# A decoder layer on one core: six state tiles instead of four, three decay tiles instead of two, and an earlier product for dt

## The chip, the core and the metric

The kernel runs on one core of a Trainium2 chip. The core has a matrix engine (PE, with its weight loads listed as PEld), a vector engine (DVE), a scalar engine (ACT), a general engine (POOL) and a queue that issues transfers (SP). Each engine works through its own list of instructions in a fixed order, and an instruction that waits holds up everything behind it on that engine. The metric is the device time of one execution in microseconds (us), the median over runs. One further execution was profiled; it gives the lines that are shown.

## The reference

Eight sequences of 512 tokens with 512 features go through three layers, each followed by a layer norm over the features:

```
x = layernorm(x + mamba(x));  x = layernorm(x + cross_attention(x, ctx));  x = layernorm(x + mixture_of_experts(x))
mamba: xn = layernorm(x);  x_main, z = split(xn @ in_proj)            # 1024 channels each
       x_main = silu(causal_conv4(x_main));  dt, Bm, Cm = split(x_main @ x_proj)      # 32, 16, 16 columns
       dt = softplus(dt @ dt_proj + b)
       h[t] = exp(A * dt[t]) * h[t-1] + dt[t] * Bm[t] * x_main[t]     # 16 states for each channel, over all t
       out = ((sum over states of h * Cm) + x_main * D) * silu(z) @ out_proj * res_scale + x
experts: a gate picks 4 of 32 experts for each token; every expert has room for 640 tokens
```

Attention has 16 heads of 32. All data are 32-bit floats.

## The kernel before

The program has three parts in a row: `layers` (the recurrent layer, attention, the gate and the shared expert, until about 4,000 us of the profiled span), `experts` and `finish`. The change is in `layers` alone.

`layers` walks over 16 chunks: 8 sequences, each in two halves of 256 tokens (`T`). A chunk has 32 steps: four pairs of channel tiles (`q`, 128 channels to a tile), for each pair four groups of four states (`g`), for each of these the two channel tiles of the pair (`ci`). One step handles 128 channels, four states and 256 tokens, and its work is spread over the engines:

- `carry` (L443, ACT) takes a state tile `h` and writes the last value of the chunk before into its first column. Tag "h" has four buffers.
- `decays` (L437, ACT) writes exp(A*dt) for the *next* step into one of the decay tiles `das`. There are two, used in turn, so the decays for step k+1 wait until the scan of step k-1 has read that tile.
- `scan` on DVE: a product dt*x*B into `h` (L449), the scan along the tokens in place (L453), and for a first half a copy of the last column (L455).
- `collect`: the product with C on DVE (L470), and on PE eight matmuls that add the states into the accumulator `py` (L474). When these are done, the buffer of `h` is free for a later step.

For every pair, `prepare` makes what its steps need: two matmuls for dt (L392) into a PSUM tile of tag "mm" (two buffers, shared by nearly all matmul results), then on ACT the parts of softplus (L402 to L408), on DVE four operations (L412 to L415), and eight DMAs on SP that spread dt and dt*x over the partitions into the two `both` tiles (L426). In the loop `prepare` for the next pair is called in step 3 of a pair (`k % 8 == 3`), and for the next chunk in step 27.

Around the steps stand, in program order: `gated` (L486, DVE, needs the finished `py` of the pair before) in the first step of a pair; `twice_x` (L490) in step 0, which loads x for the residual; `back` in steps 1 and 2 (output projection of the chunk before, residual and layer norm); `gate_x` in steps 3 to 6; for the next chunk `load_x` (L274) in step 5, `norm_x` (statistics L73, L74, then L54 to L77) in step 9, `flip_x` in step 11, `convolve` in steps 12, 15, 18 and 21 (first tap on ACT, L331, the other three taps on DVE, L339), silu (L356, L357) in step 23 and `x_proj` in step 24. The tile that `load_x` fills and the tile of `twice_x` have the same tag "xt" with one buffer. Between these, pieces of attention, gate and shared expert of the sequence before (`units`, with the score matmuls L766 and L792, the row maximum L768 on DVE and the exponentials L796 on ACT) are dealt out by weight, so that they end with the two chunks of a sequence.

The order that each engine finally sees is not the program order. A scheduler takes instructions by priority (program order) as their inputs and their tiles come free in its own model of the times, and writes one fixed list for each engine. A change of buffers or of a call's place therefore reorders all of `layers`. Below, "the built order" is this list.

Of the kernel before, what the change touches and what calls it, by code (L numbers as in the profile page):

```python
# [7 lines left out]
F32 = mybir.dt.float32  # L8
# [73 lines left out]
def layers(ctx, tc, a, x1d, filld, based, xbuf):  # L82
# [53 lines left out]
    cw = const("cw", [P, CC, 4], rows(a["conv_w"]))  # L136
    cb = const("cb", [P, CC], a["conv_b"])
    w_x = const("w_x", [P, CC, RANK + 2 * NST], rows(a["x_proj_w"]))
    w_dt = const("w_dt", [RANK, DI], a["dt_proj_w"])
    b_dt = const("b_dt", [P, CC], a["dt_proj_b"])  # L140
    dpar = const("dpar", [P, CC], a["D_param"])
    rs = const("rs", [P, 1], a["res_scale"].partition_broadcast(P))
# [15 lines left out]
    state = cp.tile([P, CC, NST // NG, NG], F32, name="l_state")  # L158
    nothing = cp.tile([P, NG, 1], F32, name="l_nothing")
    nc.gpsimd.memset(nothing, 0.0)  # L160
    das = [cp.tile([P, NG, T + 1], F32, name=f"l_da{i}") for i in range(2)]
    for da in das:
        nc.gpsimd.memset(da[:, :, 0:1], 0.0)

# [23 lines left out]
        channel_multiplier=0,  # L188
    )

    early = cp.tile([P, SC, E], F32, name="l_early")
    nc.gpsimd.iota(
        early, pattern=[[0, SC], [-1, E]], base=E, channel_multiplier=0, allow_small_or_imprecise_dtypes=True
    )
    first = cp.tile([P, SC, E], F32, name="l_first")
    nc.gpsimd.iota(
        first, pattern=[[0, SC], [CAP, E]], base=-SLOTS, channel_multiplier=0, allow_small_or_imprecise_dtypes=True
    )

    taken = cp.tile([P, SC + 1, E], F32, name="l_taken")  # L200
    nc.gpsimd.memset(taken, 0.0)
# [67 lines left out]

    piece = pieces()  # L270

    def load_x(b, t, f):
        f["xt"] = xt = p1.tile([P, NT_, D], F32, tag="xt", name="xt")
        nc.sync.dma_start(xt, a["x"][b, t * T : (t + 1) * T, :].rearrange("(j p) d -> p j d", p=P))  # L274
# [39 lines left out]
    def convolve(t, q, f):  # L314

        c0 = 2 * q
        ps = project(f, "ps_x")

        def first_tap():
            xp = p1.tile([P, 2, T + 3], F32, tag="xp", name="xp")  # L320
            if t == 0:
                nc.gpsimd.memset(xp[:, :, 0:3], 0.0)
            else:
                nc.gpsimd.tensor_copy(xp[:, :, 0:3], conv_tail[:, c0 : c0 + 2, :])
            nc.scalar.copy(xp[:, :, 3:], ps)
            if t < S // T - 1:
                nc.gpsimd.tensor_copy(conv_tail[:, c0 : c0 + 2, :], xp[:, :, T : T + 3])
            f["xs"][q] = xs = p2.tile([P, 2, T], F32, tag="xs", name="xs", bufs=6)
            for i in range(2):
                c = c0 + i  # L330
                nc.scalar.activation(  # L331
                    xs[:, i, :], xp[:, i, 0:T], AF.Identity, bias=cb[:, c : c + 1], scale=cw[:, c, 0:1]
                )

            def other_taps():
                for i in range(2):
                    acc = xs[:, i, :]
                    for k in range(1, 4):
                        nc.vector.scalar_tensor_tensor(  # L339
                            acc, xp[:, i, k : k + T], cw[:, c0 + i, k : k + 1], acc, ALU.mult, ALU.add  # L340
                        )

            return other_taps

        return first_tap
# [40 lines left out]

    def prepare(q, f):

        ps = psm.tile([P, 2, T], F32, tag="mm", name="ps_dt")
        for i in range(2):  # L390
            c = 2 * q + i
            nc.tensor.matmul(  # L392
                ps[:, i, :], w_dt[:, c * P : (c + 1) * P], f["xd"][0:RANK, :], start=True, stop=True
            )

        def exponentials():
# [5 lines left out]
                nc.scalar.activation(u[:, i, :], ps[:, i, :], AF.Abs, bias=b_dt[:, c : c + 1])  # L402
                nc.scalar.activation(dt[:, i, :], ps[:, i, :], AF.Relu, bias=b_dt[:, c : c + 1])
            nc.scalar.activation(u, u, AF.Exp, scale=-1.0)
            l = p1.tile([P, 2, T], F32, tag="l", name="l")
            nc.scalar.activation(l, u, AF.Ln, bias=1.0)
            w = dtx = p1.tile([P, 2, T], F32, tag="dtx", name="dtx")
            nc.scalar.activation(w, u, AF.Identity, bias=1.0)  # L408
# [30 lines left out]
    def carry(t, c, g):  # L439

        last = state[:, c, g].unsqueeze(2)
        h = p3.tile([P, NG, T + 1], F32, tag="h", name="h", bufs=4)
        nc.scalar.copy(h[:, :, 0:1], last if t else nothing)  # L443
        return h

# [40 lines left out]
        nc.vector.tensor_tensor(pair, pair, py, ALU.mult)  # L486

    def twice_x(b, t, f):
        f["o"] = o = p1.tile([P, NT_, D], F32, tag="xt", name="o")
        nc.sync.dma_start(o, a["x"][b, t * T : (t + 1) * T, :].rearrange("(j p) d -> p j d", p=P))  # L490
        nc.scalar.mul(o, o, 2.0)

# [51 lines left out]
    def choose(b, x2t, pl, st):  # L544
# [13 lines left out]
        square = [P, SC, G, G]  # L558
        other = gs.unsqueeze(2).to_broadcast(square)
        own = gs.unsqueeze(3).to_broadcast(square)  # L560
        eq = gm.tile(square, F32, tag="g_eq", name="g_eq")
        nc.vector.tensor_tensor(eq, other, own, ALU.is_equal)
        nc.vector.tensor_tensor(eq, eq, lower.unsqueeze(1).to_broadcast(square), ALU.mult)
        gt = gm.tile(square, F32, tag="g_gt", name="g_gt")
        nc.vector.tensor_tensor(gt, other, own, ALU.is_gt)
        nc.vector.tensor_tensor(gt, gt, eq, ALU.add)
        nc.vector.tensor_reduce(rank.unsqueeze(3), gt, AX.X, ALU.add)
# [455 lines left out]
    for i, (b, t) in enumerate(chunks):  # L1023
# [8 lines left out]
        for k, (q, g, ci) in enumerate(steps):  # L1032
# [6 lines left out]

            if k + 1 < len(steps) or after:  # L1040
                nq, ng, ni = steps[(k + 1) % len(steps)]
                decays(2 * nq + ni, ng, (f if k + 1 < len(steps) else nf)["ready", nq][0], das[(n + 1) % 2])
            scan(t, 2 * q + ci, g, f["ready", q][1], bc, das[n % 2], h)
            n += 1
            if k % 8 == 0:
                if k:
# [10 lines left out]
            if k == 7:  # L1057
                dry()
                silu(f["zs"])
            if k % 8 == 3:  # L1060
                if q + 1 < CC // 2:
                    do(prepare, q + 1, f)
                elif after:
                    do(prepare, 0, nf)
            if after:
                if k == 5:
                    load_x(*after, nf)
                if k == 9:
                    norm_x(nf)
# [349 lines left out]
```

## Time and profile before

| | |
|---|---|
| median of 3 runs | 5617.29 us (5615.69 to 5618.11) |
| profiled execution, its own time | 5620.06 us |
| its span, first to last instruction | 5617.3 us |
| mean clock granted to PE | 0.934 |
| busy over the span: PE, DVE, ACT, POOL | 87%, 77%, 46%, 10% |
| 512 steps on DVE, mean of one: L449, L453, L470 | 1.22, 2.30, 1.22 us |

In the profile's lines an operation is given by its line in the kernel, engine, names of the tiles (output <- inputs), shapes and count; after a bar follow its busy time, the mean of one in ns, and the idle time of the engine just before it with what ended it. In the chain of waits, a line such as "DVE h L449 <- PE py L474" means that the DVE instruction of L449 stood waiting, and that the PE instruction of L474 released it; then come the total in us, the number of times and the longest.

### The profile page before, as it was taken

The page shows a single profiled execution, that of the slowest core. Times are in us where ns is not written, and L with a number is a line of the kernel's source. Part 1 is how long each engine was busy: PE and PEld are TensorE (multiplying, and loading weights), DVE is VectorE, ACT ScalarE, POOL GpSimd, SP SyncE. Part 2 cuts the span into 40 slices and gives each one's busy share as a digit, 9 for nine tenths or more (in the row PEclk, how much of TensorE's full clock was granted, in tenths as well). Part 3 has the DMA queues.
Part 4 walks back from the last instruction along what each step waited for, and adds up shares of the span by engine and source line. Part 5 has one row for each costly group of instructions (what it writes and reads, how often), then busy time and mean ns, then how long its engine had stood idle before and what let it go on. Part 6 is the DMA issues. An engine that isn't in the chain of part 4 may idle for free. (4 is left out here: it accounts for less than half of the span.)

```text
span 5617.3 us, 60406 instructions
## 1 busy us (share of the span) xinstructions
PE 4888.6 (87%) x19752; PEld 2725.6 (49%) x19752; DVE 4351.5 (77%) x5738; ACT 2592.2 (46%) x5480; POOL 546.1 (10%) x424
## 2 busy tenths in 40 slices
PE   5667888888888988888888898879899999999994
PEld 3333344434433434443443443333577777777773
DVE  5988888989889998898989899854555655555554
ACT  4454555655556555565545656523122222222223
POOL 0000002001100200200010020010111111111111
PEclk8778999999999999999999999989899999999997
DMA  6777345434534534543463453431444444444444
GB/s 207 215 219 201 99 129 177 128 112 130 189 107 113 190 107 122 177 132 106 124 204 94 125 183 110 115 118 45 137 124 126 124 124 119 125 126 124 120 117 138
DMA packets 560426, 769.83 MB, mean 137 GB/s; under 512 B 135754, under 2 KB 268394, under 8 KB 560112
## 3 DMA queue, kind: packets, MB, share of 16 engines
q1 hardware_dynamic: 522608, 680.70, 40.2%
q0 software_dynamic: 33280, 76.90, 7.0%
q10 hardware_dynamic: 4224, 8.39, 0.4%
q8 instruction: 156, 2.56, 0.2%
q14 instruction: 158, 1.29, 0.1%
HBM read 508.68 MB, written 165.05 MB: 120 GB/s over the span
## 5 line engine op out<-in xcount | busy, mean ns | idle before, releaser
L437 ACT ACTIVATE l_da<-both,l_aneg 128x256 f32<-128x256 f32 x2048 | 888.4, 499 | 801.8 <-DVE h L453 759.7
L453 DVE TENSOR_TENSOR_SCAN h<-l_da,h 128x1028 f32<-128x1028 f32 x512 | 1171.2, 2295 | 48.5 <-ACT h L443 26.4
L474 PE MATMUL py<-h,l_twice 128*64 128x256 f32 x4096 | 628.1, 420 | 217.4 <-DVE h L470 217.3
L449 DVE TENSOR_TENSOR h<-both,bc 128x1024 f32<-128x1024 f32 x512 | 619.2, 1216 | 97.2 <-PE py L474 45.4
L470 DVE TENSOR_TENSOR h<-h,bc 128x1024 f32<-128x1024 f32 x512 | 623.5, 1220 | 6.0
L474 PEld LDWEIGHTS py<-h,l_twice 128*64 128x64 f32 x4096 | 295.3, 147 | 587.6 <-DVE h L470 260.7
L766 PE MATMUL ps_s<-l_ka,l_qa 64*128 64x512 f32 x1024 | 317.1, 699 | 142.9 <-DVE mx L768 142.7
L1199 PE MATMUL ps_h<-xT,w 128*128 128x320 f32 x1536 | 435.6, 433 | 0.0
L1279 POOL DMA_INDIRECT based<-y,xe x160 | 250.5, 1565 | 1317.2 <-ACT y L1302 579.9
L768 DVE TENSOR_REDUCE mx<-ps_s 128x2 f32<-128x1024 f32 x256 | 310.8, 1217 | 83.7 <-PE ps_s L766 82.9
L1220 DVE TENSOR_TENSOR hT<-ps_h,p 128x320 f32<-128x320 f32 x128 | 62.9, 492 | 374.7 <-PE ps_h L1199 374.6
L1199 PEld LDWEIGHTS ps_h<-xT,w 128*128 128x128 f32 x1536 | 292.4, 191 | 118.4 <-issue 0.8
L792 PE MATMUL ps_t<-l_qa,l_ka 64*128 64x512 f32 x1024 | 302.0, 654 | 15.8 <-ACT eT L796 11.9
L796 ACT ACTIVATE eT<-ps_t 128x1024 f32<-128x1024 f32 x256 | 259.1, 1013 | 111.9 <-PE ps_t L792 111.5
L808 PE MATMUL po<-eT,l_va 128*64 128x512 f32 x1024 | 279.2, 623 | 23.0 <-ACT raw L820 19.0
L1199 PE MATMUL ps_h<-t,s 128*128 128x320 f32 x1024 | 286.1, 432 | 0.0
L641 POOL DMA_INDIRECT xbuf<-x2t,dest x128 | 216.7, 1693 | 622.1 <-DVE dest L635 583.7
L305 PE MATMUL ps_z<-xnT,wm 128*128 128x256 f32 x1024 | 246.3, 395 | 31.2 <-DMA wm<-in_in_proj_w 28.4
L503 PE MATMUL po<-wm,zs 128*128 128x512 f32 x512 | 246.7, 634 | 13.0 <-DMA wm<-in_out_proj_w 8.5
L703 PE MATMUL ps_p<-x2T,wa 128*128 128x512 f32 x512 | 244.7, 627 | 11.1 <-DVE hT L883 9.1
L305 PE MATMUL ps_x<-xnT,wm 128*128 128x256 f32 x1024 | 245.3, 393 | 1.4 <-ACT xnT L294 1.1
L305 PEld LDWEIGHTS ps_z<-xnT,wm 128*128 128x128 f32 x1024 | 196.2, 196 | 83.7 <-ACT l_da L437 27.1
(225 smaller groups left out, 7397.0 us busy)
## 6 DMA issues: line engine op xcount, KB each, us to landing
bc<-scr SPq DMA_DIRECT2D x1024, 128.0 KB
w<-in_w SPq DMA_DIRECT2D x96, 1024.0 KB
wm<-in_in_proj_w SPq DMA_DIRECT2D x128, 512.0 KB
xbuf<-zero SPq DMA_DIRECT2D x32, 1362.5 KB
xe<-xbuf SPq DMA_DIRECT2D x32, 1362.5 KB
both<-dt SPq DMA_DIRECT2D x256, 128.0 KB
both<-dtx SPq DMA_DIRECT2D x256, 128.0 KB
wm<-in_out_proj_w SPq DMA_DIRECT2D x64, 512.0 KB
```

Source lines behind the costliest of these rows:

```text
L305: nc.tensor.matmul(ps[:, i, :], w[:, dc, i * P : (i + 1) * P], f["xnT"][:, dc, :], start=(dc == 0), stop=(dc == DC - 1),)
L437: nc.scalar.activation(da[:, n, 1:], dt[:, c % 2, j, :], AF.Exp, scale=aneg[:, c, j, g, m : m + 1])
L449: nc.vector.tensor_tensor(steps, dtx[:, c % 2].unsqueeze(2).to_broadcast([P, 2, NG // 2, T]), bc[0], ALU.mult)
L453: nc.vector.tensor_tensor_scan(flat, da.rearrange("p n t -> p (n t)"), flat, 0.0, ALU.mult, ALU.add)
L470: nc.vector.tensor_tensor(steps, steps, bc[1], ALU.mult)
L474: nc.tensor.matmul(py[j * HP : (j + 1) * HP, c % 2, :], twice, h[:, j * 2 + m, 1:], start=False, stop=(s == (NST // NG - 1, NG // 2 - 1, 1)),)
L766: nc.tensor.matmul(ps[:, j, :], qa[r, lt * P : (lt + 1) * P], ka[r, :], start=True, stop=True)
L768: return lambda: nc.vector.tensor_reduce(mx[:, lt, :].unsqueeze(2), ps, AX.X, ALU.max) and None
L792: nc.tensor.matmul(ps[:, j, :], ka[r, kc * P : (kc + 1) * P], qa[r, :], start=True, stop=True)
L796: nc.scalar.activation(eT, ps, AF.Exp)
L808: nc.tensor.matmul(po[j * 2 * HD : (j + 1) * 2 * HD, :], va[:, kc, i, j * HD : (j + 2) * HD], eT[:, j, :], start=(kc == 0), stop=(kc == SC ...
L1199: nc.tensor.matmul(ps, w[:, n, r * P : (r + 1) * P], x[:, n, :], start=not more and n == 0, stop=n == 1, skip_group_check=more,)
```

## The change

- `h` has six buffers, `das` three tiles.
- `twice_x` uses a tile of its own (tag "o"), so that x for the next chunk and x for the residual no longer share one.
- `prepare` for the next pair is called in the first step of a pair (0, 8, 16), and for the next chunk in step 26; `load_x` in step 3.
- The weights for dt are no longer held in SBUF as a whole. A generator loads the 32x256 piece for a pair, one pair ahead, into two buffers: 65 DMAs on SP instead of one.
- To make room: `xs` (the convolved x) has five buffers instead of six; the tile `l` of softplus shares its one buffer with `xp`, the input of the convolution; two tiles of the gate share the buffers of tag "row"; two constant tables of the gate are kept once and read repeatedly.

```diff
@@ -136,7 +136,6 @@
     cw = const("cw", [P, CC, 4], rows(a["conv_w"]))
     cb = const("cb", [P, CC], a["conv_b"])
     w_x = const("w_x", [P, CC, RANK + 2 * NST], rows(a["x_proj_w"]))
-    w_dt = const("w_dt", [RANK, DI], a["dt_proj_w"])
     b_dt = const("b_dt", [P, CC], a["dt_proj_b"])
     dpar = const("dpar", [P, CC], a["D_param"])
     rs = const("rs", [P, 1], a["res_scale"].partition_broadcast(P))
@@ -158,7 +157,7 @@
     state = cp.tile([P, CC, NST // NG, NG], F32, name="l_state")
     nothing = cp.tile([P, NG, 1], F32, name="l_nothing")
     nc.gpsimd.memset(nothing, 0.0)
-    das = [cp.tile([P, NG, T + 1], F32, name=f"l_da{i}") for i in range(2)]
+    das = [cp.tile([P, NG, T + 1], F32, name=f"l_da{i}") for i in range(3)]
     for da in das:
         nc.gpsimd.memset(da[:, :, 0:1], 0.0)
 
@@ -188,14 +187,12 @@
         channel_multiplier=0,
     )
 
-    early = cp.tile([P, SC, E], F32, name="l_early")
-    nc.gpsimd.iota(
-        early, pattern=[[0, SC], [-1, E]], base=E, channel_multiplier=0, allow_small_or_imprecise_dtypes=True
-    )
-    first = cp.tile([P, SC, E], F32, name="l_first")
-    nc.gpsimd.iota(
-        first, pattern=[[0, SC], [CAP, E]], base=-SLOTS, channel_multiplier=0, allow_small_or_imprecise_dtypes=True
-    )
+    early = cp.tile([P, E], F32, name="l_early")
+    nc.gpsimd.iota(early, pattern=[[-1, E]], base=E, channel_multiplier=0, allow_small_or_imprecise_dtypes=True)
+    early = early.unsqueeze(1).to_broadcast([P, SC, E])
+    first = cp.tile([P, E], F32, name="l_first")
+    nc.gpsimd.iota(first, pattern=[[CAP, E]], base=-SLOTS, channel_multiplier=0, allow_small_or_imprecise_dtypes=True)
+    first = first.unsqueeze(1).to_broadcast([P, SC, E])
 
     taken = cp.tile([P, SC + 1, E], F32, name="l_taken")
     nc.gpsimd.memset(taken, 0.0)
@@ -269,6 +266,19 @@
 
     piece = pieces()
 
+    def dts():
+
+        got = None
+        for n in range(B * (S // T) * CC // 2 + 1):
+            q = n % (CC // 2)
+            nxt = p2.tile([RANK, 2 * P], F32, tag="wdt", name="wdt")
+            nc.sync.dma_start(nxt, a["dt_proj_w"][:, 2 * q * P : 2 * (q + 1) * P])
+            if got is not None:
+                yield got
+            got = nxt
+
+    w_dt = dts()
+
     def load_x(b, t, f):
         f["xt"] = xt = p1.tile([P, NT_, D], F32, tag="xt", name="xt")
         nc.sync.dma_start(xt, a["x"][b, t * T : (t + 1) * T, :].rearrange("(j p) d -> p j d", p=P))
@@ -325,7 +335,7 @@
             nc.scalar.copy(xp[:, :, 3:], ps)
             if t < S // T - 1:
                 nc.gpsimd.tensor_copy(conv_tail[:, c0 : c0 + 2, :], xp[:, :, T : T + 3])
-            f["xs"][q] = xs = p2.tile([P, 2, T], F32, tag="xs", name="xs", bufs=6)
+            f["xs"][q] = xs = p2.tile([P, 2, T], F32, tag="xs", name="xs", bufs=5)
             for i in range(2):
                 c = c0 + i
                 nc.scalar.activation(
@@ -386,11 +396,11 @@
 
     def prepare(q, f):
 
+        w = next(w_dt)
         ps = psm.tile([P, 2, T], F32, tag="mm", name="ps_dt")
         for i in range(2):
-            c = 2 * q + i
             nc.tensor.matmul(
-                ps[:, i, :], w_dt[:, c * P : (c + 1) * P], f["xd"][0:RANK, :], start=True, stop=True
+                ps[:, i, :], w[:, i * P : (i + 1) * P], f["xd"][0:RANK, :], start=True, stop=True
             )
 
         def exponentials():
@@ -402,7 +412,7 @@
                 nc.scalar.activation(u[:, i, :], ps[:, i, :], AF.Abs, bias=b_dt[:, c : c + 1])
                 nc.scalar.activation(dt[:, i, :], ps[:, i, :], AF.Relu, bias=b_dt[:, c : c + 1])
             nc.scalar.activation(u, u, AF.Exp, scale=-1.0)
-            l = p1.tile([P, 2, T], F32, tag="l", name="l")
+            l = p1.tile([P, 2, T + 3], F32, tag="xp", name="l")[:, :, 0:T]
             nc.scalar.activation(l, u, AF.Ln, bias=1.0)
             w = dtx = p1.tile([P, 2, T], F32, tag="dtx", name="dtx")
             nc.scalar.activation(w, u, AF.Identity, bias=1.0)
@@ -439,7 +449,7 @@
     def carry(t, c, g):
 
         last = state[:, c, g].unsqueeze(2)
-        h = p3.tile([P, NG, T + 1], F32, tag="h", name="h", bufs=4)
+        h = p3.tile([P, NG, T + 1], F32, tag="h", name="h", bufs=6)
         nc.scalar.copy(h[:, :, 0:1], last if t else nothing)
         return h
 
@@ -486,7 +496,7 @@
         nc.vector.tensor_tensor(pair, pair, py, ALU.mult)
 
     def twice_x(b, t, f):
-        f["o"] = o = p1.tile([P, NT_, D], F32, tag="xt", name="o")
+        f["o"] = o = p1.tile([P, NT_, D], F32, tag="o", name="o")
         nc.sync.dma_start(o, a["x"][b, t * T : (t + 1) * T, :].rearrange("(j p) d -> p j d", p=P))
         nc.scalar.mul(o, o, 2.0)
 
@@ -558,10 +568,10 @@
         square = [P, SC, G, G]
         other = gs.unsqueeze(2).to_broadcast(square)
         own = gs.unsqueeze(3).to_broadcast(square)
-        eq = gm.tile(square, F32, tag="g_eq", name="g_eq")
+        both = p3.tile([P, D], F32, tag="row", name="g_eq").rearrange("p (n j g h) -> p n j g h", n=2, j=SC, g=G)
+        eq, gt = both[:, 0], both[:, 1]
         nc.vector.tensor_tensor(eq, other, own, ALU.is_equal)
         nc.vector.tensor_tensor(eq, eq, lower.unsqueeze(1).to_broadcast(square), ALU.mult)
-        gt = gm.tile(square, F32, tag="g_gt", name="g_gt")
         nc.vector.tensor_tensor(gt, other, own, ALU.is_gt)
         nc.vector.tensor_tensor(gt, gt, eq, ALU.add)
         nc.vector.tensor_reduce(rank.unsqueeze(3), gt, AX.X, ALU.add)
@@ -1039,8 +1049,8 @@
 
             if k + 1 < len(steps) or after:
                 nq, ng, ni = steps[(k + 1) % len(steps)]
-                decays(2 * nq + ni, ng, (f if k + 1 < len(steps) else nf)["ready", nq][0], das[(n + 1) % 2])
-            scan(t, 2 * q + ci, g, f["ready", q][1], bc, das[n % 2], h)
+                decays(2 * nq + ni, ng, (f if k + 1 < len(steps) else nf)["ready", nq][0], das[(n + 1) % 3])
+            scan(t, 2 * q + ci, g, f["ready", q][1], bc, das[n % 3], h)
             n += 1
             if k % 8 == 0:
                 if k:
@@ -1057,13 +1067,12 @@
             if k == 7:
                 dry()
                 silu(f["zs"])
-            if k % 8 == 3:
-                if q + 1 < CC // 2:
-                    do(prepare, q + 1, f)
-                elif after:
-                    do(prepare, 0, nf)
+            if k in (0, 8, 16):
+                do(prepare, q + 1, f)
+            if k == 26 and after:
+                do(prepare, 0, nf)
             if after:
-                if k == 5:
+                if k == 3:
                     load_x(*after, nf)
                 if k == 9:
                     norm_x(nf)
```

## The prediction

> **What bounds the kernel now.** I read the page first: engines' busy time, then the span in slices.
>
> ```profile
> PE 4888.6 (87%) x19752; PEld 2725.6 (49%) x19752; DVE 4351.5 (77%) x5738; ACT 2592.2 (46%) x5480; POOL 546.1 (10%) x424
> ...
> PE   5667888888888988888888898879899999999994
> DVE  5988888989889998898989899854555655555554
> ```
>
> PE leads over the span, but DVE leads in the first 25 slices, which hold all that the change touches. So next come busy times by stretch (columns PE, PEld, DVE, ACT, POOL), cut where the chunks begin to run evenly and where they end.
>
> ```profile
> 200.00:3590.00 3390.00, 2918.08 (x11872) 1394.44 (x11868) 3059.75 (x3488) 1910.81 (x4053) 242.27 (x187) 0.93 0.49 144
> ```
>
> DVE works 3059.75 of 3390 us (90.3%) and is idle 330.25; PE is busy for 86%, ACT for 56%. No DVE work is removed, so the gain must come out of the 330 us. Third view: DVE's waits in this window, which sum to 291 us; the other 39 are short gaps between dependent instructions.
>
> ```profile
> DVE h L449 <- PE py L474: 45.4, 27, 3.7
> DVE zs L486 <- PE py L474: 39.5, 17, 4.3
> DVE st L73 <- DMA xt<-in_x: 36.4, 14, 9.5
> DVE xs L339 <- ACT xs L331: 33.0, 21, 4.7
> DVE dtx L412 <- ACT dtx L408: 27.0, 7, 5.2
> DVE h L453 <- ACT h L443: 26.4, 16, 2.0
> DVE h L449 <- DMA both<-dtx: 23.0, 13, 7.1
> ```
>
> The change aims at all but the fourth: state tiles at lines 1, 2 and 6, the x tile at line 3, the early product at 5 and 7. The same view for ACT shows why many large waits there are worth nothing by themselves:
>
> ```profile
> ACT l_da L437 <- DVE h L453: 705.0, 298, 5.3
> ```
>
> ACT waits for a decay tile that DVE's scan frees, but DVE waits for decays only 4.0 us in all (L453 <- L437): ACT is ahead, and a third tile can gain 4 at most.
>
> **The change part by part.** Counts of what stands between two instructions are from the built orders; durations are of the profiled execution (5620.06 us, 2.8 above the median). "Cover" is DVE work between a request and its use.
>
> *The x tile: -20.* The timeline of chunk 6 shows the load and its use (start, duration):
>
> ```profile
> 1437.30 0.37 SPq L274 DMA_DIRECT2D xt<-in_x  x1
> ...
> 1442.59 1.29 DVE L73 BATCH_NORM_STATS2 st<-xt 128x6 f32<-128x512 f32 x2 [3.51 <-DMA xt<-in_x]
> ```
>
> Issue to use takes 5.3 us here, 4.6 in chunk 3. With its own tile the load is no longer held by the residual's. In 11 of 15 chunks its issue then stands 1.9 to 2.3 us of DVE work ahead of L73, if SP comes to it only there; its tile is released 5.5 us ahead, which hides it wholly if SP is free. So between 11 x (4.95-2.1) = 31 remains (gain 5) and nothing (gain 36); SP's place between is not in the trace, and I take the middle.
>
> *The early product: -18.* L412 waits for the end of softplus 27.0 us, 7 times, all at step 7. Called three steps earlier, five such places stay tight, of which I leave 5 us in all: -22 (10 to 27). Behind L415 come the copies that L449 needs. With nothing between, the price is in chunk 15:
>
> ```profile
> 3560.90 0.69 DVE L414 TENSOR_TENSOR dt<-dt,l 128x512 f32<-128x512 f32 x1
> ...
> 3561.66 2.69 SPq L426 DMA_DIRECT2D both<-dt  x4
> 3564.45 2.55 SPq L426 DMA_DIRECT2D both<-dtx  x4
> 3569.39 1.23 DVE L449 TENSOR_TENSOR h<-both,bc 128x1024 f32<-128x1024 f32 x1 [7.08 <-DMA both<-dtx]
> ```
>
> The copies of dtx queue on SP behind those of dt, so the trip is 7.8 us from the end of L414 (3561.59). For a chunk's second pair (step 8) the cover between L415 and L449 is 3.0 us before and 12.7 or 18.6 after: both waits that I find there, 23.0 and 7.0 (L449 <- PE ps_s L766, one of several releases), go: -30. But the next chunk's first pair is now prepared one step earlier in name and later in the built order. Ahead of the odd chunks 3 to 15 the order becomes L413, L414, L768, L415, L768, L449: after L414 stand 1.22 + 0.69 + 1.22 = 3.1 us, so 4.7 are bare, 7 x 4.7 = 33; even chunks fall from 8.8 to 6.0 us of cover, up to 7 x 1.8 = 13 more, which I keep for the range. Sum -22 - 30 + 34 = -18 (-24 to +7).
>
> *Six state tiles: -61.* Between the last product (L470) in a tile and the next L449 in the same tile, 123 of 508 places had under 15 DVE instructions; after, none. Yet L474 must also get its turn on PE, where it stands behind attention's matmuls, which wait for DVE (L766 <- mx L768: 136.8 us). Of L449s that sit less than 1 us of DVE work behind their releasing matmuls in PE's list, 203 become 184. So L449's 45.4 falls by less than half: -20 (0 to -45). The column that ACT carries in (L453 <- L443, 26.4) hangs on the same L474: a third, -8 (0 to -26). L486 needs the pair's last sums. Its cover after the pair's last L470 was 1.3 to 2.0 us in 14 places, 2 in each pair of chunks; after it is at least 12 there. Two or three early waits stay: -33 (0 to -39).
>
> *Shared and smaller buffers: +23.* `l` now waits until the taps have read `xp`. That puts softplus's Ln behind silu or taps 15 times, with 15 more table loads on ACT. A load takes 1283 ns in the trace (L356), so 19 us of ACT, which idles 1479 of the 3390: hidden, save that L413 then waits some 0.6 us 15 times: +9 (0 to 28). The Trainium skill ("ScalarE: Activation LUTs", "Table sets: the hidden batching unit") says to batch activations by table set, because each change of set pays a load; it speaks against this sharing, by its rule all 19 us would count, and the sum below would be 10 higher. At the end of odd chunks the gate's small operations and the row maximum now stand in one dependent run: some 2 us x 7 = +14 (0 to 21). Five `xs` tiles cost no more where L339 already waits.
>
> *Third decay tile: -4.* *64 more SP issues: 0.* They take 0.37 to 0.6 us each by L274 and its like, 24 to 38 us of SP; each piece is asked for a pair ahead, some 50 us before its use. If they push the copies of L426 instead, they cost up to 38. The row maximum, taps and all else keep their counts: 0.
>
> Sum: -20 - 18 - 61 + 9 + 14 - 4 = -80. PE is 86% busy in this stage, and DVE made 80 us faster asks PE and ACT for the same work sooner: what DVE gains partly returns as L449 <- L474 and as waits for scores (L768 <- L766, 13.1 now). I let a third return (an estimate, from PE's 14% of room against DVE's 10): -53. 5620.1 - 53 = 5567 profiled, 5564 median.
>
> **The rivals.**
>
> *Waits trade places: within 0.2% (11 us, about what a measurement of this kernel can tell from no change), 5606 to 5628, say 5615.* For it: DVE and PE are both near 90%, and chains between them (L470, L474, L768, L766) are unchanged. Against it: L73 and step 8 wait for transfers, not PE, and their cover does grow.
>
> *Slower: DVE runs dry at chunk boundaries.* The next chunk's x_proj, softplus and copies would end too late for step 0. Price: the trip with one L768 as cover, 7.8 - 1.2 = 6.6, and two table loads in front, 2.6: 9.2 at 7 odd boundaries, and 7.8 + 2.6 - 6.0 = 4.4 at 8 even ones: 64 + 35 = 99. The wait takes the place of my +33, +9 and +14, and state tiles gain nothing, as DVE stands for dt and not for them: -20 - 52 - 4 + 99 = +23, so 5643 profiled, 5640 median. It decides from 76/15 = 5.1 us per boundary; my own sum has 57/15 = 3.8. For it: the order at odd boundaries is shown; against it: at even ones 6.0 of 7.8 us stay covered.
>
> *Much faster: all waits on state tiles go.* -36 for x, -18, -111 (45.4 + 26.4 + 39.5), -4: -169; with a third returned -113, so 5504 median. For it: no tile is asked for again within 15 instructions. Against it: PE's place of L474.
>
> **How the numbers follow.** My forecast 0.43 (5530 to 5606), no difference 0.13, slower 0.27, much faster 0.17; so faster 0.60. For 8 in 10 the range runs from 5490 (below the third rival's point; without any return it would be 5448) to 5660 (above the slower rival's 5640, with some 13 us more at even boundaries and part of the 38 of SP).
>
> **What would show it.** Right: L73 <- xt under 25 us, L486 <- L474 near 6, no L449 <- both at step 8, and 4 to 5 us of it at step 0 of odd chunks; L449 <- L474 near 25. Wrong: waits of over 5 us per boundary for L408, L406 or `both`; L449 <- L474 at 45 or more; or L768 and L503's waits growing by tens of us, which would mean that PE has become the bound.

## The result, and the profile after

The changed kernel takes 5697.92 us (median of 4, 5697.12 to 5707.0) against 5617.7: a ratio of 1.0146, 95% interval 1.0129 to 1.0164, so 80 us slower. The forecast was 5564 us, in a range from 5490 to 5660. The profiled execution has a span of 5695.4 us.

From `load_x` on the changed file is ten lines longer: L449, L453, L470, L474, L486 and L512 of before are L459, L463, L480, L484, L496 and L522 now, L412 to L415 are L422 to L425, L381 and L426 are L391 and L436, L766 and L768 are L776 and L778, L703 and L883 are L713 and L893. The carry, L443 before, is L453 now.

The page first: busy time of each engine, then PE and DVE in 40 slices.

```profile
PE 4894.4 (86%) x19752; PEld 2727.8 (48%) x19752; DVE 4355.8 (76%) x5738; ACT 2612.6 (46%) x5495; POOL 558.2 (10%) x425
...
PE   5667888888888988888898888889799999999994
DVE  5998888988988888898988889873455555555554
```

Busy times and counts are as before to 6 us on PE and 4 on DVE, so neither got more work; ACT's 20 us more are 15 more table loads (150 against 135). DVE's high stretch is the same work over a longer time. What DVE waits for, from 200 to 3660 us:

```profile
DVE h L459 <- DMA bc<-scr: 51.2, 13, 9.3
DVE o L522 <- PE po L513: 40.5, 12, 4.2
DVE mx L778 <- PE ps_s L776: 37.3, 29, 2.2
DVE h L463 <- ACT h L453: 34.9, 23, 4.4
DVE hT L893 <- PE ps_p L713: 34.2, 18, 4.6
DVE h L459 <- PE py L484: 33.4, 24, 2.7
DVE h L459 <- DMA both<-dtx: 27.3, 7, 4.8
DVE xs L349 <- ACT xs L341: 25.2, 22, 2.6
DVE dtx L422 <- ACT dtx L418: 21.6, 8, 3.5
DVE zs L496 <- PE py L484: 13.8, 15, 3.1
DVE g_m L560 <- ACT g_sc L559: 10.8, 6, 1.8
DVE st L73 <- DMA xt<-in_x: 10.1, 8, 2.5
```

The seven waits that led before summed to 231 us and are now 166 (33.4 + 13.8 + 10.1 + 25.2 + 21.6 + 34.9 + 27.3), 65 less. Five that were small before come to 174 (`bc`, `po`, `ps_s`, `ps_p` into hT, and the gate's L560), where before they were 25 (2.3 + 7.8 + 13.1 + 1.8 + 0). The change removed waits, and more came in their place.

Where they came, the starts of the scans tell. A chunk's length is taken here from its first product (L449 or L459) on DVE to that of the next chunk, as a mean over chunks 2 to 13, even ones (a sequence's first half) and odd ones apart; idle is DVE's time between instructions where the gap is over 0.2 us, its part in the last step of all chunks and in step 0, with the wait ahead of the step's first product counted to step 0 (8.9 us of it, ahead of the very first chunk, are the same in both kernels).

| | even | odd | pair | idle at last step | at step 0 |
|---|---|---|---|---|---|
| before | 227.4 | 244.2 | 471.6 | 2.1 | 11.0 |
| after | 224.0 | 260.1 | 484.1 | 75.3 | 36.2 |

The pair of chunks is 12.5 us longer. The six pairs of chunks 2 to 13 make 75 us of the loss and the first pair 5 more; the last two chunks, with what follows them until the experts' first matmul, take 3 less. Even chunks became 3.4 us shorter, odd ones 16 longer, and at chunk ends and starts DVE idles 98 us more (75.3 + 36.2 - 13.1). That is more than the whole loss; everywhere else between the first product and the last DVE idles 27 us less (gaps over 0.2 us in all: 308 before, 379 after). Of the 98 us, 65 lie at the ends of odd chunks and 35 at the ends of even ones, 27 of these in the wait for `both` in the list above; inside step 0 it is 2 less.

Such an end, as busy time of PE, PEld, DVE, ACT and POOL in one stretch. Before, from the gate's first operations in chunk 13 to the first scans of chunk 14:

```profile
3229.00:3290.00 61.00, 58.85 (x197) 25.28 (x196) 59.45 (x106) 29.46 (x62) 13.68 (x7) 0.98 0.43 129
```

After, the same place:

```profile
3319.00:3357.00 38.00, 38.00 (x111) 17.22 (x111) 25.66 (x82) 19.24 (x34) 1.22 (x1) 1.00 0.39 119
```

Before, PE and DVE were both at 96% or more, side by side. After, PE is at 100% for 38 us, most of it with the shared expert's matmuls (L713), and DVE at 68%. What DVE does there, from its timeline (start, duration):

```profile
3317.79 1.22 DVE L480 TENSOR_TENSOR h<-h,bc 128x1024 f32<-128x1024 f32 x1
3318.93 2.46 DVE L349 SCALAR_TENSOR_TENSOR xs<-xp,l_cw,xs 128x256 f32<-128x256 f32 x6
3321.31 0.28 DVE L556 TENSOR_REDUCE g_m<-ps_l 128x4 f32<-128x128 f32 x1
...
3338.01 0.69 DVE L893 TENSOR_TENSOR hT<-hT,ps_p 128x512 f32<-128x512 f32 x1 [1.75 <-PE ps_p L713]
...
3342.36 0.69 DVE L422 SCALAR_TENSOR_TENSOR dtx<-dtx,u 128x512 f32<-128x512 f32 x1 [3.46 <-ACT dtx L418]
...
3345.08 0.69 DVE L425 TENSOR_TENSOR dtx<-dt,xs 128x512 f32<-128x512 f32 x1
...
3355.41 2.35 DVE L459 TENSOR_TENSOR h<-both,bc 128x1024 f32<-128x1024 f32 x2
```

The last scan's product (L480) is done at 3319, the next scan belongs to the next chunk and comes after 3357. Between lie the next chunk's last taps, the whole gate in small dependent operations, hT and the next chunk's dt, one chain through PE, ACT and DVE without a scan to fill its gaps. In the built order of before, 6 scans of an odd chunk still stand behind the last taps and the gate's first operation, and 1 behind the last operation for the next dt (L415); in the changed one 0, 0 and 0. These three counts (taps, gate, dt) are given below where they bear on an experiment.

### The profile page after: what moved, and what is told of

It reads as the page before. It is cut to its first block, busy times and chain, and to the rows that moved or that the text cites. A ratio compares the mean times of both kernels' runs of the same rounds, so it can differ in the third digit from the quotient of the medians.

```text
span 5695.4 us, 60561 instructions
## 1 busy us (share of the span) xinstructions
PE 4894.4 (86%) x19752; PEld 2727.8 (48%) x19752; DVE 4355.8 (76%) x5738; ACT 2612.6 (46%) x5495; POOL 558.2 (10%) x425
## 3 DMA queue, kind: packets, MB, share of 16 engines
q1 hardware_dynamic: 525680, 682.70, 39.2%
## 5 line engine op out<-in xcount | busy, mean ns | idle before, releaser
L463 DVE TENSOR_TENSOR_SCAN h<-l_da,h 128x1028 f32<-128x1028 f32 x512 | 1169.7, 2295 | 53.3 <-ACT h L453 39.7
L484 PE MATMUL py<-h,l_twice 128*64 128x256 f32 x4096 | 640.9, 426 | 191.5 <-DVE h L480 191.4
L459 DVE TENSOR_TENSOR h<-both,bc 128x1024 f32<-128x1024 f32 x512 | 619.2, 1219 | 126.2 <-DMA bc<-scr 60.1
L480 DVE TENSOR_TENSOR h<-h,bc 128x1024 f32<-128x1024 f32 x512 | 622.2, 1221 | 5.9
L484 PEld LDWEIGHTS py<-h,l_twice 128*64 128x64 f32 x4096 | 305.1, 149 | 556.0 <-DVE h L480 232.1
L776 PE MATMUL ps_s<-l_ka,l_qa 64*128 64x512 f32 x1024 | 324.9, 715 | 163.4 <-DVE mx L778 163.2
L778 DVE TENSOR_REDUCE mx<-ps_s 128x2 f32<-128x1024 f32 x256 | 310.6, 1218 | 110.1 <-PE ps_s L776 109.2
L776 PEld LDWEIGHTS ps_s<-l_ka,l_qa 64*128 64x128 f32 x1024 | 88.4, 204 | 311.2 <-DVE mx L778 241.3
L713 PE MATMUL ps_p<-x2T,wa 128*128 128x512 f32 x512 | 235.2, 612 | 1.7 <-ACT x2T L880 1.4
```

The lines of the kernel that those rows point to most:

```text
L459: nc.vector.tensor_tensor(steps, dtx[:, c % 2].unsqueeze(2).to_broadcast([P, 2, NG // 2, T]), bc[0], ALU.mult)
L463: nc.vector.tensor_tensor_scan(flat, da.rearrange("p n t -> p (n t)"), flat, 0.0, ALU.mult, ALU.add)
L480: nc.vector.tensor_tensor(steps, steps, bc[1], ALU.mult)
L484: nc.tensor.matmul(py[j * HP : (j + 1) * HP, c % 2, :], twice, h[:, j * 2 + m, 1:], start=False, stop=(s == (NST // NG - 1, NG // 2 - 1, 1)),)
L776: nc.tensor.matmul(ps[:, j, :], qa[r, lt * P : (lt + 1) * P], ka[r, :], start=True, stop=True)
L778: return lambda: nc.vector.tensor_reduce(mx[:, lt, :].unsqueeze(2), ps, AX.X, ALU.max) and None
```

## The experiments

**Theories.** *Tail*: six tiles let the scheduler put scans ahead of the work on which the next scans depend, and ends of odd chunks are left as a bare chain. *Sharing*: the buffers given up (l, xs, the gate's tiles) cost. *Spread*: transfers and a busy PE, anywhere. All runs are ratios to the kernel before on the same chip (medians 5617 to 5621).

**The two large parts, alone and together.** `h6_alone` is `bufs=4` to `bufs=6` for `h`; `prep_alone` is

```diff
-            if k % 8 == 3:
-                if q + 1 < CC // 2:
-                    do(prepare, q + 1, f)
-                elif after:
-                    do(prepare, 0, nf)
+            if k in (0, 8, 16):
+                do(prepare, q + 1, f)
+            if k == 26 and after:
+                do(prepare, 0, nf)
```

`h6_prep` has both.

> The kernel before with six state tiles and nothing else. In its built order the last taps and the first operation of the gate still have 7 scans of the odd chunk left beside them (6 before, 0 after), but the last operation for the next chunk's dt stands behind the last scan (1 scan left before, 0 after). Tail theory (the loss of the change sits at the end of odd chunks, where steps that ran ahead leave nothing beside the taps, the gate and the shared expert; it takes the six tiles and the early product together): a part of the loss only, 5600 to 5650 us. Sharing theory (the loss comes from l in xp's buffer, five xs buffers and the gate in the row buffers): faster, about 5565 to 5600 us, since six tiles were forecast to give 61 before returns.

Measured: 5762.98 us, 1.0253 (1.0239 to 1.0267), 144 us slower, the dearest part of all; both theories missed. DVE's waits from 200 to 3660 us:

```profile
DVE dtx L412 <- ACT dtx L408: 99.6, 26, 6.8
DVE xs L339 <- ACT xs L331: 99.1, 32, 5.1
DVE h L449 <- DMA both<-dtx: 81.2, 25, 7.9
```

The two waits on state tiles that six tiles should end are gone from the top, but `dt` is waited for at 26 pair starts (7 times before) and its copies 25 times: with prepare in step 3 the scans now reach the end of a pair before dt for the next is ready. L412 stands at steps 8, 16, 24 and 32 of a chunk, behind all the scans of its pair; before it stood at 8, 15, 23 and 31. The counts are 7, 7, 0, and of 64.3 us of idle time at the last step 56.3 lie at the ends of even chunks: the ends of odd chunks are not bare (8.0 us of it), and dt comes late at many pairs. How the 144 us divide was not tested further.

> The kernel before with only the product for dt called in the first step of a pair and in step 26. In its built order 2 scans of the odd chunk are left after the last tap and the first operation of the gate (6 before, 0 after). Tail theory: a loss at the end of odd chunks of about a half of the whole, against the gain of some 30 us at steps 7 and 8: 5610 to 5650 us. Sharing theory: faster, 5580 to 5600 us (22 and 30 us gone, 34 back at step 0).

Measured: 5655.07 us, 1.0065 (1.0051 to 1.0079), 36 us slower. The copies at step 8 are waited for no longer, as forecast; L412's wait stays at 29.2 us (27.0 before), and the statistics' wait for x rises from 36.4 to 56.9, `po` from 7.8 to 27.1, `bc` from 2.3 to 26.9. The idle time at chunk ends is as before (0.0 and 10.8 us), though 2, 2 and 1 scans are left there: its loss is of the spread kind, and not that of the tail.

> Both parts together on the kernel before, with no buffer shared, w_dt kept whole, two decay tiles and x in the shared tile. The built order has 0 scans left after taps, gate and dt of odd chunks, as the changed kernel has. Tail theory: most of the loss is here, 5680 to 5710 us, with DVE idle by 10 us or more at the end of each odd chunk. Sharing theory: the forecast gain, 5560 to 5600 us. If it lies between the two parts' sum and the changed kernel, both have a share.

Measured: 5663.9 us, 1.0081 (1.0068 to 1.0095), counts 0, 0, 0. The early product cures 99 us of what the six tiles cost alone. Even chunks take 219.4 us (227.4 before), odd ones 259.7 (244.2), idle at the last step 77.6: the tail is here, with no buffer shared. The time lies below the tail theory's 5680 to 5710; even chunks gain 8 us each, which the theory had not counted. Against `prep_alone`, which differs by the two tiles alone, even chunks fall from 229.6 to 219.4 us and odd ones rise from 247.1 to 259.7: the gain that six tiles were to bring, and its loss at the tail.

**Which call of the early product.** `prep_0_8_16` has the first condition of the diff above, with the second at step 27; `prep_26` has only the second, and the first at steps 3, 11 and 19.

> The kernel before with prepare called in steps 0, 8 and 16 for the next pair; the call for the next chunk stays in step 27. Built order: 2 scans behind the last taps and the gate of odd chunks, as with the whole early product (5655). If the calls in steps 0, 8, 16 are what costs: 5645 to 5670 us. If the call for the next chunk costs: 5590 to 5625.

Measured: 5648.82 us, 1.0048 (1.0036 to 1.0060).

> The kernel before with only the call for the next chunk moved from step 27 to 26. Built order: 6 scans behind taps and gate as before, 2 behind the next chunk's dt (1 before). Tail theory: no loss, 5600 to 5622 us. If this call is what costs in the early product: 5640 to 5660.

Measured: 5626.25 us, 1.0011 (1.0002 to 1.0020), 4 us above what the tail theory had allowed. The calls in steps 0, 8 and 16 cost 29 of the 36 us, the one in step 26 some 7. In the first, `po` (54.1 us) and `bc` (42.4) lead DVE's waits.

**The x tile.** `o_load` gives the residual's x its own tag and calls `load_x` in step 3; `o_alone` is the tag alone; `after_xt` takes both back in the changed kernel.

```diff
-        f["o"] = o = p1.tile([P, NT_, D], F32, tag="xt", name="o")
+        f["o"] = o = p1.tile([P, NT_, D], F32, tag="o", name="o")
...
-                if k == 5:
+                if k == 3:
                     load_x(*after, nf)
```

> The kernel before with a tile of its own for the residual's x and the load for the next chunk in step 3. The order at the chunk ends is as before. Both theories: the wait of the statistics for x (36 us in 14 places) falls by half or more, and the time by 5 to 36 us: 5580 to 5612 us, 5597 by my term. If the time does not move, these waits only made room for others.

Measured: 5633.06 us, 1.0023 (1.0013 to 1.0033), 14 us slower. The wait of L73 for x has gone from DVE's waits altogether (36.4 before), and L449 <- `both` rose from 23.0 to 65.1 us. The timelines of DVE at the same place of chunk 6 show how. Before:

```profile
1438.38 0.69 DVE L415 TENSOR_TENSOR dtx<-dt,xs 128x512 f32<-128x512 f32 x1
1442.59 1.29 DVE L73 BATCH_NORM_STATS2 st<-xt 128x6 f32<-128x512 f32 x2 [3.51 <-DMA xt<-in_x]
...
1445.89 2.36 DVE L449 TENSOR_TENSOR h<-both,bc 128x1024 f32<-128x1024 f32 x2
```

`o_load`:

```profile
1443.05 0.69 DVE L415 TENSOR_TENSOR dtx<-dt,xs 128x512 f32<-128x512 f32 x1
1451.37 2.36 DVE L449 TENSOR_TENSOR h<-both,bc 128x1024 f32<-128x1024 f32 x2 [7.63 <-DMA both<-dtx]
```

From L415 to L449 it is 7.5 us before and 8.3 in `o_load`, where it is the trip of the copies and nothing else. Before, the wait for x, and the 3 us of statistics behind it, ran inside that trip and cost next to nothing here; moved elsewhere, they leave the trip bare. This was read at one place; that it makes up the whole 14 us is argued from the rise of the wait for `both`.

> The kernel before with a tile of its own for the residual's x, the load of x left in step 5. With the load in step 3 as well, the statistics' wait went, but the copies to both, which had run beside it, then stood bare, and the time rose by 14 us. If it is the earlier place of the statistics that uncovers the copies: the tile alone does little, 5605 to 5625 us. If freeing the load from the residual's tile is enough to move the statistics: 5625 to 5640.

Measured: 5630.83 us, 1.0014 (1.0005 to 1.0023). The tile alone is enough: `both` is waited for 58.1 us. That the call's place matters was not borne out.

> The changed kernel with the residual's x back in the tile xt and the load for the next chunk back in step 5. On the kernel before, the tile and the earlier load cost 14 us, since the statistics' wait had covered the copies to both. If that cost is part of the changed kernel's excess over the two larger parts together (5698 against 5664 us): 5675 to 5690 us. If the early product gives the copies other cover, the x tile gains here: 5700 to 5730 us.

Measured: 5677.52 us, 1.0105 (1.0089 to 1.0121): the x tile and the earlier load cost 20 us within the change too.

**Fewer tiles, and the shared buffers.** `after_h4` sets `bufs=6` of `h` in the changed kernel to 4. `h6_prep_shared` is `h6_prep` with

```diff
-    das = [cp.tile([P, NG, T + 1], F32, name=f"l_da{i}") for i in range(2)]
+    das = [cp.tile([P, NG, T + 1], F32, name=f"l_da{i}") for i in range(3)]
...
-            f["xs"][q] = xs = p2.tile([P, 2, T], F32, tag="xs", name="xs", bufs=6)
+            f["xs"][q] = xs = p2.tile([P, 2, T], F32, tag="xs", name="xs", bufs=5)
...
-            l = p1.tile([P, 2, T], F32, tag="l", name="l")
+            l = p1.tile([P, 2, T + 3], F32, tag="xp", name="l")[:, :, 0:T]
```

> The changed kernel with four state tiles. Built order: 2 scans left after taps and gate of odd chunks, as in the kernel with the early product alone, which took 5655. Tail theory, and what the early product alone showed: 5640 to 5680 us, some 20 to 50 below the changed kernel. Theory that the six tiles help and the shared buffers cost: slower than the changed kernel, above 5700.

Measured: 5676.92 us, 1.0103 (1.0087 to 1.0118); counts 2, 2, 1, idle at the last step 0.2 us. Six tiles cost 21 us within the change: four bring the tail back into order and lengthen even chunks from 224.0 to 232.4, while odd ones fall from 260.1 to 246.6. With the ends in order again the kernel is still 59 us slower than before, so the tail is not the whole loss.

> Six tiles and the early product on the kernel before (5664 us), with l in xp's buffer, five xs buffers and three decay tiles as well; x, w_dt and the gate's tiles as before. If the shared buffers are part of the rest of the loss (my forecast had 9 us for l, 0 for xs, a gain of 4 for the decays): 5668 to 5685 us. If not: 5655 to 5668, and the rest lies in the x tile (20 us by after_xt), w_dt and the gate.

Measured: 5674.31 us, 1.0105 (1.0090 to 1.0119), 10 above `h6_prep`; the two intervals overlap. The shared buffers and the third decay tile account for some 10 us, not for 80. The steps from before to after are then 36 (early product), 9 (six tiles on it), 10 (sharing and third decay tile), 20 (x), and some 5 left for w_dt by pieces and the gate's tiles, which had no run of their own.

**Filling the tail.** If the bare chain is the loss, giving it scans must win the loss back. The pieces of attention, gate and shared expert are dealt out by one condition:

```diff
-                while side and spent + sum(own[:at]) <= whole * at / len(own):
+                while side and spent + sum(own[:at]) <= whole * (at + 6) / len(own):
```

> The changed kernel with the pieces of attention, gate and shared expert dealt out six steps earlier (one number in the loop), everything else as changed. In its built order 6 scans of the odd chunk stand behind the last taps again (0 in the changed kernel, 6 before) and 11 behind the gate's first operation (0; 6). Tail theory: the odd chunk's end fills up, its 12 us of extra idle DVE time go, 7 times, and the time falls by 50 to 90 us, to 5605 to 5650. If the loss were spread over the chunk (transfers, shared buffers, a busy PE), dealing earlier would move it by less than 20 us: above 5678.

> The control: the kernel before with the same one number changed. Its odd chunks already end with 6 scans beside taps and gate (8 and 16 now). Tail theory: little to gain, 5600 to 5630 us. If it gained as much as the changed kernel does (50 us or more), the earlier dealing would be good by itself and would say nothing of the change.

Measured: 5816.85 us (1.0357, 1.0343 to 1.0371) and 5802.27 us (1.0321, 1.0307 to 1.0335). Both missed. Odd chunks fell to 241.3 and 238.3 us as they should, but the six steps' worth also comes at once at the start of a sequence, and even chunks rose to 263.2 and 265.4. So the shift was restricted to second halves, and made to grow from nothing to six steps: `(at + 6 * max(0, at - len(steps)) / len(steps))` in place of `(at + 6)`.

> The changed kernel with the pieces of attention, gate and shared expert dealt out earlier in the second half of a sequence alone: by nothing at its start, growing to six steps at its end. First halves are as in the changed kernel. Built order: 5 scans behind the last taps of odd chunks, 8 behind the gate's first operation (0 and 0 in the changed kernel). With six steps in both halves the odd chunks fell from 260 to 240 us, and the even ones rose from 222 to 261. Tail theory: odd chunks at 240 to 250 us, even ones at 222, so 60 to 100 us less over 7 pairs: 5590 to 5640. If the odd chunks fell there only because work had left them for the even ones: 5680 to 5710.

Measured: 5671.82 us, 1.0088 (1.0074 to 1.0102), 26 below the changed kernel but not in the expected range. Counts 5, 8, 0. The ramp also moves work from even chunks into odd ones (212.9 and 268.5 us), so from here on only pairs compare: 481.4 us, against 484.1 in the changed kernel. Idle at the last step fell from 75.3 to 7.9 us as it should, but at step 0 it rose from 36.2 to 97.8. The start of chunk 14, DVE and then SP:

```profile
3335.88 0.69 DVE L425 TENSOR_TENSOR dtx<-dt,xs 128x512 f32<-128x512 f32 x1
3336.49 0.68 DVE L496 TENSOR_TENSOR zs<-zs,py 128x512 f32<-128x512 f32 x1
3346.78 2.36 DVE L459 TENSOR_TENSOR h<-both,bc 128x1024 f32<-128x1024 f32 x2 [9.62 <-DMA both<-dtx]
```

```profile
3335.91 2.71 SPq L436 DMA_DIRECT2D both<-dt  x4
3338.71 4.06 SPq L436 DMA_DIRECT2D both<-dtx  x4
```

The gate and the taps have scans again, but dt has none (the third count is still 0), and the trip of its copies takes their place as the bare chain.

> Six state tiles and the early product on the kernel before, and the same ramp of six steps in the second halves. Without the ramp even chunks gain 8 us each and odd ones lose 15 against the kernel before (5664 us). Built order: 5 scans behind the last taps, 9 behind the gate's first operation. Tail theory: even chunks stay at 218, odd ones come near the 244.5 of before: some 45 to 90 us below 5664, so 5575 to 5620, perhaps below both kernels. Otherwise: 5650 to 5680.

> The control: the kernel before with the ramp alone. It has 6 scans behind the last taps and 6 behind the gate's first operation; with the ramp 8 and 9. Tail theory: odd chunks have little to gain, 5605 to 5640 us. A gain of 40 us or more would mean that the ramp is good by itself.

Measured: 5695.68 us (1.0128, 1.0113 to 1.0144) and 5672.28 us (1.0091, 1.0076 to 1.0106). The first is 32 slower than `h6_prep`, a miss, with 101.8 us idle at step 0 for the same reason. The ramp by itself costs the kernel before 52 us, above the 5640 expected at most.

The last step was to give dt scans as well. `after_ramp6_early3` calls everything for the next chunk, except `load_x`, three steps sooner:

```diff
-            if k == 26 and after:
+            if k == 23 and after:
...
-                if k == 9:
+                if k == 6:
...
-                if k in (12, 15, 18, 21):
+                if k in (9, 12, 15, 18):
...
-                if k == 24:
+                if k == 21:
```

> The changed kernel with the ramp of six steps in second halves, and with the next chunk's statistics, transposes, convolution, silu, x_proj and prepare all called three steps earlier. Built order at the end of odd chunks: 7 scans behind the last taps, 8 behind the gate's first operation, 3 behind the last operation for the next chunk's dt (after_ramp6: 5, 8, 0; changed kernel: 0, 0, 0; before: 6, 6, 1). Tail theory, completed by the dt chain: the 98 us of idle time at step 0 and the rest at step 31 fall to 20 and 50: 60 to 100 us below after_ramp6's 5672, so 5570 to 5620. If the total of DVE's idle time is set by something else (PE at 86%, where the wait only shows), the time stays within 25 us of 5672, with the idle time in a third place.

Measured: 5612.61 us (median of 11), 0.9988 (0.9979 to 0.9996); counts 7, 8, 3. Idle at step 0 falls to 12.6 us, at the last step to 3.5: 95 us less at the ends, and the time is 85 us below the changed kernel and 7 below the kernel before. The pair is down from 484.1 to 471.9 us (471.6 before), so 73 of the 82 us between the two profiled spans lie in the six pairs of chunks 2 to 13. Busy times at the end of chunk 13, DVE third:

```profile
3234.00:3284.00 50.00, 48.89 (x181) 22.21 (x181) 47.89 (x75) 27.88 (x61) 14.16 (x10) 1.00 0.50 166
```

PE and DVE are side by side again, at 98% and 96%.

> The control: the kernel before (four state tiles, prepare in steps 3, 11, 19) with the ramp of six steps and the next chunk's calls three steps earlier, prepare for it in step 24. With the ramp alone it took 5672. Built order: 8 scans behind taps of odd chunks, 10 behind the gate's first operation, 4 behind the next chunk's dt. Tail theory: nothing was missing at its chunk ends, so no gain over the kernel before: 5630 to 5680 us. If the schedule is good by itself: 5560 to 5610, below the changed kernel with it (5613).

Measured: 5674.63 us, 1.0093 (1.0077 to 1.0108). The same schedule costs the kernel before 53 us, whose ends had scans already, and gives the changed kernel 85. So it is a repair of this loss, and no gain by itself. Its own 53 us are not idle time at the ends (11.5 and 9.1 us); where they come from was not tested.

Last, the x tile again, with the ends filled: `tag="o"` back to `tag="xt"` in `after_ramp6_early3`.

> The changed kernel with the ramp and the earlier calls (5613 us), and the residual's x back in the tile xt; the load stays in step 3, three steps ahead of the statistics. In the changed kernel itself the tile back in xt, and the load in step 5, gave 20 us. If that cost holds with filled chunk ends: 5585 to 5602 us, faster than both kernels. If it came from the stretched chunk ends alone: 5608 to 5620; if the statistics now wait for x again: 5620 to 5650.

Measured: 5648.95 us, 1.0049 (1.0035 to 1.0062). A miss: with filled ends the x tile saves 36 us, where it cost 20 in the changed kernel. Its sign depends on what stands around it; the two edits are not quite the same, since `after_xt` also moved the load from step 3 to step 5. Here `dtx` is waited for 33.6 us at L422; why the shared tile brings that was not tested.

## Why the prediction was wrong, step by step

*The bound and the place* were right: DVE in the first 25 slices, and its idle time decides.

*The x tile, forecast -20.* The wait fell as forecast, from 36.4 to 10.1 us, yet the time rose by 14 alone and by 20 within the change. The failed step is taking L73's wait at its full length: it ran beside the trip of the copies to `both`, which the forecast counted a second time as 23.0 and 7.0 us.

*The early product, forecast -18.* The copies at step 8 went and the new wait at step 0 came as worked out (27.3 us in 7 places; forecast 33, entered in the sum as 34). L412 kept 21.6 of 27.0 us instead of 5. What the forecast had at nothing were `bc` and `po`. Some of `bc`'s loads stand in SP's queue behind a store that waits. Chunk 12, SP and DVE:

```profile
2915.81 0.37 SPq L525 DMA_DIRECT2D x1d<-o  x1
2916.22 0.48 SPq L391 DMA_DIRECT2D bc<-scr  x1
```

```profile
2917.46 2.36 DVE L459 TENSOR_TENSOR h<-both,bc 128x1024 f32<-128x1024 f32 x2 [3.23 <-DMA bc<-scr]
```

The store L525 waits 2.8 us for the layer norm's last operation on ACT, and the load for the next scan waits behind it. The same stands at step 6 of chunks 4, 6, 8 and 10; these five waits are 18.3 of the 51.2 us. SP was counted by its 38 us of extra issues, not by what stands in front of what. The part alone costs 36 us.

*Six state tiles, forecast -61.* L459 <- L484 fell by 12 us (forecast 20) and L496 by 26 (forecast 33). The carry's wait rose from 26.4 to 34.9 (forecast -8), but not by the tiles: with six tiles alone no scan waits for it, with the early product alone scans wait 39.2 us. In the changed kernel the copy stands on ACT behind silu and a table load at step 12 of odd chunks:

```profile
2701.70 1.91 ACT L366 ACTIVATE zs<-zs 128x2048 f32<-128x2048 f32 x1
2703.63 1.28 ACT L367 ACT_TABLE_LOAD   x1
2704.92 1.02 ACT L806 ACTIVATE eT<-ps_t 128x1024 f32<-128x1024 f32 x1
2705.84 0.19 ACT L453 COPY h<-l_state 128x4 f32<-128x4 f32 x1
```

and the scan waited 4.37 us, as it did at step 12 of six more chunks. The gain that was forecast is there in even chunks, 10.2 us each from `prep_alone` to `h6_prep`; odd ones lose 12.6 at their ends. Added to the early product, six tiles cost 9 us where 61 were to be gained.

*The end of odd chunks, forecast +14 for the gate's dependent run and +9 for Ln: the step that failed.* The run of small operations was seen in the built order, and priced as its own gaps. That no scan was left beside it, nor beside taps, hT and dt, was not counted, though the same order showed it (6, 6 and 1 scans became 0, 0 and 0). Idle at the last step rose by 73 us, 65 of them at the ends of odd chunks, in place of that 14 and 9. This is where the gain of the six tiles went. It is not the only step that failed: with these ends in order `prep_alone` is still 36 us slower and `after_h4` 59, near the 36 of the early product and the 20 of the x tile, which were forecast at -18 and -20.

The 9 for Ln had the wrong cause. ACT has 150 table loads against 135, as counted, but `h6_prep`, where `l` keeps its own buffer, has 154: the loads come with the order and not with the sharing. The Trainium skill ("ScalarE: Activation LUTs", "Table sets: the hidden batching unit") says to batch activations by table set, and so spoke against such loads. Sharing `l`, together with `xs` and the third decay tile, costs some 10 us (the two intervals overlap), so the sharing is not where the 80 us went.

*The third returned* fails as a model: what came back (149 us in the five waits above) is over twice what went (65).

*The rivals.* The slower one named the place, DVE dry at chunk boundaries, and priced it at 99 us against the measured 98 of extra idle time there. That the two agree is luck: it put 64 us ahead of the odd chunks and 35 ahead of the even ones, and measured were 35 and 65. Its mechanism, copies and dt late for step 0, holds for the 27 us of `both` ahead of the odd chunks. Ahead of the even ones, in the stretch shown, the first product (L459 at 3355.41) waits for no copy, and DVE's idle time is that of hT (5.4 us), dt (3.5) and the gate (1.8). It put its 99 in place of 57 us that the forecast had there, so that its 5640 us still kept 76 us of gains elsewhere; 27 were measured. It had a chance of 0.27, and the range ended 38 us below the time.

## What to carry to other kernels

More buffers for the bound engine's own steps let a scheduler run these ahead; look in the built order at what is then left for the end of each stage, and count the bound engine's large operations behind every late chain (side work, and the next stage's inputs). A wait is worth its length only if nothing else waits beside it: before crediting one, ask which transfer or chain is running under it. Move the producers of the next stage ahead together with the buffers: here the same schedule change was worth 85 us with the change and cost 53 without it, and the two together were 7 us faster than the kernel before.

## What the runs showed of the hardware

PE's busy time is not a count of its work: `h6_alone` has the same 19752 matmuls as before and 4950.9 us of busy time against 4888.6, at a granted clock of 0.921 against 0.934. In proportion to the clock it would be 4888.6 x 0.934 / 0.921 = 4957.6, but the proportion does not hold throughout: `after_ramp6_early3`, at 0.939, has 4885.9, where it would give 4862.6. Some part of the 144 us of `h6_alone` may be the clock's; no run tells it apart. `after_deal6` had 0.922; the other profiled executions had 0.926 to 0.939. The changed kernel had 0.932 and 6 us more of PE's busy time than before, too little to explain 80 us.
